# Layer-norm statistics of the last stage by bn_stats and Newton steps, and the output copy on ScalarE

## The chip, the core and the metric

The kernel runs on one core of a Trainium2 chip. The metric is the device time of one execution in microseconds (us), from runs on the chip. TensorE (PE) does matrix products and transposes, VectorE (DVE) elementwise work and sums, ScalarE (ACT) elementwise functions and copies, GpSimd (POOL) and SyncE (SP) issue DMAs. Each engine works off its own list of instructions in order and waits on semaphores of the others.

## The reference, cut to what matters

Two networks follow each other on a float32 tensor of shape (4, 64, 256, 256). The last stage of the kernel computes the second network's column attention and its feed-forward block. For every pixel `x` is a vector of E = 64 channels:

```
def ln(x, g, b):
    m = x.mean(-1); v = mean((x - m) ** 2, -1)
    return (x - m) / sqrt(v + 1e-5) * g + b

h = x + lin_attn(ln(x, cn_g, cn_b), col_wq, col_wk, col_wv, col_wo)
      # q, k = elu(.) + 1, one number per head and pixel; q over its mean, k over its sum;
      # k^T v over a column's 256 rows, then q times that, then col_wo
out = h + w2 @ gelu(w1 @ ln(h, fn_g, fn_b) + b1) + b2
```

So each pixel is normalized twice: once ahead of the scores `q` and `k`, once ahead of the feed-forward. The scales and shifts `g`, `b` and the first centring are folded into the weights (`cwt`, `cgt`, `w1`, `b1`), so the kernel needs the reciprocal root `rs` of the variance for the scores, and `(x - m) * rs` for the feed-forward.

## The kernel before, in words

The earlier stages compute the first network and the row attention; the change does not touch them. The last one, `stage_d`, goes over 32 tiles `h` (4 images, 8 groups of 32 columns). A tile has 128 partitions, `h[p, c, a, e]`: column `c` of 32, row half `a` of 2, channel `e` of 64; partition and `a` make the row. Tiles come from `hd` by four DMAs of SP, two tiles ahead, four buffers.

Three tiles are in work at once, in a loop over `n`:

- `scores(n + 1)`: eight passes `r`. `up(r)` turns four columns' `h` on TensorE (L1252), ScalarE copies them to `xT` (L1254), `score` multiplies with `cwt` (L1261), `back` turns the results on VectorE (L1266) into `qp`. Ahead of pass 0 and after pass 3 `spread` computes half the tile's sums of squares. At the end `rstd` gives `rs`; `qp` times `rs` plus the bias (L1291, L1292) goes through `feature`: the minimum with 0 on VectorE (`fe`, L711), the exp on ScalarE (L712); then `f` (L1300) and `kz` (L1302).
- `result(n)`: the product of `kz` and `h` (L1313), its sums `zm` and `z` (L1325, L1327), `zn` (L1332), turned (L1335, L1337), through `mix` (L718 to L726) to `bdm` (L1341). Then twice four matmuls of the bias (L1347) and of `bdm` (L1350), and eight adds into `h` in place (L1353), four for each row half `a`. Then for each half `hf` of the columns `spread` and `rstd`, and the products `xf` (L1362).
- the feed-forward of tile `n - 1`, in eight passes of four columns: `turn` two passes ahead (`xf` turned, L1372, copied by ScalarE to `xfT`, L1374), `first` one pass ahead (four matmuls with `w1`, L1383, and Gelu on ScalarE into `hg`, L1385), `second` (`h` turned into the bank, L1397, products with `w2` on top, L1400, and a copy with the bias `b2` to `st`, L1401). `st` is written with a step of 32 words. After eight passes four DMAs of GpSimd write `st` to the output.

`spread` makes, for 16 pixels of 64 channels per partition at a time: the sum (L1223), the centred values `xc` (L1225), the squares on ScalarE (L1227) and their sum (L1231). `rstd` takes a root on ScalarE (L1236) and a reciprocal on VectorE (L1238). ScalarE holds one table of functions at a time: the root, the exp and the Gelu each need another, and a load (ACT_TABLE_LOAD) stands in its list at each change.

TensorE's order is written out by hand in the loop (`tc.manual_schedule`); a scheduler orders the lists of the other engines by its own costs when the program is built. Matmul results go to six PSUM banks (`mm`) and two (`sm`); a bank is used again when the engine that reads it is done.

Of the kernel before, what the change touches and what calls it, by code (L numbers as in the profile page):

```python
# [8 lines left out]

F32 = mybir.dt.float32  # L10
AF = mybir.ActivationFunctionType
ALU = mybir.AluOpType
AX = mybir.AxisListType

C, H, W = 64, 256, 256
HW = H * W
NPAIR = H // 2
EPS = 1e-5
LN_S = 1.0 / C
# [230 lines left out]
def kernel(ctx: ExitStack, tc: tile.TileContext, x, packs, fd, out, off):  # L250
    nc = tc.nc
    B = x.shape[0]
    V, S, T, G, SY = nc.vector, nc.scalar, nc.tensor, nc.gpsimd, nc.sync
# [24 lines left out]
    eps_t = const.tile([128, 1], F32, name="eps_t")  # L278
# [18 lines left out]
    def bc(ap, n):  # L297

        return ap.unsqueeze(2).to_broadcast([ap.shape[0], ap.shape[1], n])
# [10 lines left out]
    def layernorm(pool, src, xc, g, bufs=None):  # L310

        s1 = pool.tile([128, g], F32, tag="ln_s", name="ln_s")
        V.tensor_reduce(s1, src, AX.X, ALU.add)
        V.scalar_tensor_tensor(xc, bc(s1, C), -LN_S, src, ALU.mult, ALU.add)  # L314
        sq = pool.tile([128, g, C], F32, tag="ln_sq", name="ln_sq", bufs=bufs)
        S.activation(sq, xc, AF.Square)  # L316
        s2 = pool.tile([128, g], F32, tag="ln_v", name="ln_v")
        V.tensor_reduce(s2, sq, AX.X, ALU.add)  # L318
        s3 = pool.tile([128, g], F32, tag="ln_d", name="ln_d")
        S.activation(s3, s2, AF.Sqrt, bias=eps_t, scale=LN_S)  # L320
        s4 = pool.tile([128, g], F32, tag="ln_r", name="ln_r")
        V.reciprocal(s4, s3)
        V.tensor_tensor(xc, xc, bc(s4, C), ALU.mult)


    sp1 = ctx.enter_context(ExitStack())
    p = sp1.enter_context(tc.tile_pool(name="pst", bufs=2))
    p1 = sp1.enter_context(tc.tile_pool(name="pst1", bufs=1))
# [14 lines left out]
    K = load_pack(p1, "s")  # L343
# [837 lines left out]
    def stage_d():  # L1181
        with ExitStack() as cs:
            p = cs.enter_context(tc.tile_pool(name="pd", bufs=2))
            p1 = cs.enter_context(tc.tile_pool(name="pd1", bufs=1))
            K = load_pack(p1, "d")
            cwg, cbq, cgg = attn_weights(p1, "col", K)

            t = mm()
# [5 lines left out]
            t = mm()  # L1194
# [6 lines left out]
            t = mm()  # L1201
# [12 lines left out]
                        SY.dma_start(h[:, 16 * j:16 * j + 16, rh, :], hd[b, rh * 128:(rh + 1) * 128, :, 2 * g + j, :])  # L1214
                return h

            def spread(h, ks, v):

                xcs, sqs = [], []
                for k in ks:  # L1220
                    src = h[:, 8 * k:8 * k + 8].rearrange("p c a e -> p (c a) e")
                    s1 = p.tile([128, 16], F32, tag="ln_s", name="ln_s")
                    V.tensor_reduce(s1, src, AX.X, ALU.add)  # L1223
                    xc = p.tile([128, 16, C], F32, tag="xc", name="xc")
                    V.scalar_tensor_tensor(xc, bc(s1, C), -LN_S, src, ALU.mult, ALU.add)  # L1225
                    sq = p.tile([128, 16, C], F32, tag="ln_sq", name="ln_sq")
                    S.activation(sq, xc, AF.Square)  # L1227
                    xcs.append(xc)
                    sqs.append(sq)
                for i, k in enumerate(ks):  # L1230
                    V.tensor_reduce(v[:, 16 * i:16 * i + 16], sqs[i], AX.X, ALU.add)  # L1231
                return xcs

            def rstd(v, n):
                s3 = p.tile([128, n], F32, tag="ln_d", name="ln_d")
                S.activation(s3, v, AF.Sqrt, bias=eps_t, scale=LN_S)  # L1236
                s4 = p.tile([128, n], F32, tag="ln_r", name="ln_r")
                V.reciprocal(s4, s3)  # L1238
                return s4

            def scores(n):
                h = hs[n]
                qp = p1.tile([128, 32, 32], F32, name="qp")
                v1 = p1.tile([128, 64], F32, name="v1")

                def up(r):
                    t = mm()  # L1250
                    for i in range(4):
                        T.transpose(t[:, i * 128:(i + 1) * 128], h[:, r * 4 + i].rearrange("p a e -> p (a e)"), ident)  # L1252
                    xT = p.tile([128, 512], F32, name="xT")
                    S.copy(xT, t)  # L1254
                    return xT

                def score(r, xT, qk):


                    for g in range(4):  # L1260
                        T.matmul(qk[g * 32:(g + 1) * 32, r % 4 * 128:r % 4 * 128 + 128], cwt, xT.rearrange("p (c n) -> p c n", c=4)[:, :, g * 32:(g + 1) * 32],  # L1261
                                 start=True, stop=True)

                def back(k, qk):

                    V.transpose(qp[:, k * 16:k * 16 + 16].rearrange("p c m -> p (c m)"), qk)  # L1266

                xT = up(0)
                yield
                yield  # L1270
                qk = sm()
                for r in range(8):
                    if r == 0:
                        spread(h, (0, 1), v1[:, 0:32])
                    if r == 4:
                        back(0, qk)
                        qk = sm()
                    score(r, xT, qk)
                    if r < 7:
                        xT = up(r + 1)  # L1280
                    if r == 3:
                        spread(h, (2, 3), v1[:, 32:64])
                    yield
                    if r == 1:
                        yield
                        yield

                back(1, qk)
                rs = rstd(v1, 64)
                u = qp[:, :, 0:16].rearrange("p c (r k) -> p c r k", r=2)  # L1290
                V.tensor_tensor(u, u, bc4(rs, 2, 8), ALU.mult)  # L1291
                V.tensor_tensor(u, u, cbq.unsqueeze(1).unsqueeze(1).to_broadcast([128, 32, 2, 8]), ALU.add)  # L1292
                e = feature(p1, u, [128, 32, 2, 8])
                yield
                f = p1.tile([128, 2, 2, 32, 4], F32, name="f")
                uv = u.rearrange("p c r k -> p r c k")
                ev = e.rearrange("p c r k -> p r c k")
                for rh in (0, 1):
                    for k in (0, 1):
                        V.scalar_tensor_tensor(f[:, rh, k], uv[:, rh, :, k * 4:k * 4 + 4], 1.0, ev[:, rh, :, k * 4:k * 4 + 4], ALU.add, ALU.max)  # L1300
                kz = p1.tile([128, 2, 128], F32, name="kz")
                V.tensor_tensor(kz.rearrange("p r (c h) -> p r c h", h=4), f[:, :, 1], rs.rearrange("p (c r) -> p r c", r=2).unsqueeze(3).to_broadcast([128, 2, 32, 4]), ALU.mult)  # L1302
                fks[n] = f, kz

            def result(n):
                h = hs[n]
# [46 lines left out]
                        V.tensor_tensor(hh, ts[g].rearrange("p (c e) -> p c e", c=8), hh, ALU.add)  # L1353
                    yield
                for hf in (0, 1):
                    v2 = p.tile([128, 32], F32, name="v2")
                    xcs = spread(h, (2 * hf, 2 * hf + 1), v2)
                    yield
                    rs = rstd(v2, 32)
                    for k in (0, 1):  # L1360
                        xf = p.tile([128, 8, 2, C], F32, name="xf", bufs=6)
                        V.tensor_tensor(xf.rearrange("p c a e -> p (c a) e"), xcs[k], bc(rs[:, k * 16:k * 16 + 16], C), ALU.mult)  # L1362
                        xfs[n, 2 * hf + k] = xf
                    yield
# [23 lines left out]
            def second(i):  # L1388

                n, r = divmod(i, 8)  # L1390
                h, hg = hs[n], hgs.pop(i)
                if r == 0:
                    sts[n] = p.tile([128, 128, 32], F32, name="st")
                st = sts[n]
                y = mm()
                for k in range(4):
                    T.matmul(y[:, k * 128:(k + 1) * 128], h[:, r * 4 + k].rearrange("p a e -> p (a e)"), ident, is_transpose=True, start=(k == 0), stop=False, skip_group_check=True)  # L1397
                for k in (0, 1):
                    for rh in (0, 1):
                        T.matmul(y[rh * 64:(rh + 1) * 64, :], w2[:, k, :], hg[k * 2 + rh], start=False, stop=(k == 1), skip_group_check=True)  # L1400
                V.tensor_scalar(st[:, :, 4 * r:4 * r + 4].rearrange("p r c -> p c r"), y.rearrange("p (c r) -> p c r", c=4), K("b2"), None, ALU.add)  # L1401
                if r == 7:
                    b, g = seq[n]
                    for q in (0, 1):
                        for rh in (0, 1):
                            y0 = rh * 128 + q * 64
                            G.dma_start(out[b, :, y0:y0 + 64, g * 32:g * 32 + 32], sts[n][rh * 64:(rh + 1) * 64, q * 64:(q + 1) * 64])  # L1407
                    del hs[n]
# [46 lines left out]
```

## Time and profile before

| what | value |
|---|---|
| times of three runs | 8467.74, 8469.86, 8471.41 us; median 8469.86 |
| span of the profiled execution | 8468.2 us, 1.7 below the median of the runs |
| granted TensorE clock, mean | 0.976 |
| TensorE busy | 7969.8 us, 94% |
| VectorE busy | 5829.9 us, 69% |
| ScalarE busy | 4723.4 us, 56% |
| last stage | from about 6351 us to the end |
| first and last `z` (L1327) of its 32 tiles | 6398.3 and 8367.5 us |

The profile is of one execution. Its views: the page; busy time by stretches; groups of instructions by line, shape and operation, with busy time, mean and idle time before them; waits by who waited for whom; the chain of work that ended last; the timeline, where a row gives start and duration, and `xN` merges N instructions. A duration reaches from an instruction's start to its end, and on VectorE and ScalarE the next often starts a little before that end. Lines (L1223) are those of the kernel before.

### The profile page before, as it was taken

What the parts mean: (1) busy time and instruction counts of PE and PEld (TensorE: products, weight loads), DVE (VectorE), ACT (ScalarE), POOL (GpSimd) and SP (SyncE); (2) the same over time, 40 slices, a digit from 0 to 9 for tenths busy, and PEclk for the clock granted to TensorE, in tenths of its full rate; (3) what the DMA queues carried; (4) which work ended last, traced back from release to release, by engine and by line L of the source; (5) the groups of instructions that cost most, each with busy time, mean ns of one, the idle gap of its engine ahead of it and who ended that gap; (6) DMA issues with size and microseconds to landing.
All of it is one profiled execution on the core that took longest, in us unless ns stands there. A gap on an engine that the chain in (4) does not pass through costs nothing.

```text
span 8468.2 us, 143522 instructions
## 1 busy us (share of the span) xinstructions
PE 7969.8 (94%) x57518; PEld 4144.7 (49%) x57518; DVE 5829.9 (69%) x8506; ACT 4723.4 (56%) x8297; POOL 1077.1 (13%) x1764
## 2 busy tenths in 40 slices
PE   8999998799999998999999999999987999999998
PEld 6877777344444443333333345555553444444443
DVE  7777775577777773222222278888877888888886
ACT  4466554455555553222222267777765777777776
POOL 1122221122222221000000001111110010010111
PEclk9999999799999999999999999999997999999999
DMA  7788886899999998888888866666642333333332
GB/s 164 169 217 218 214 209 164 278 391 389 388 389 392 394 383 303 299 296 295 298 298 299 278 208 187 193 187 194 186 130 64 64 76 60 68 73 60 72 69 40
DMA packets 1258505, 1832.50 MB, mean 216 GB/s; under 512 B 335600, under 2 KB 1040112, under 8 KB 1196656
## 3 DMA queue, kind: packets, MB, share of 16 engines
q1 hardware_dynamic: 1053296, 1034.63, 40.8%
q0 software_dynamic: 204544, 788.69, 29.3%
q8 instruction: 456, 7.47, 0.4%
q14 instruction: 209, 1.71, 0.1%
HBM read 967.65 MB, written 788.53 MB: 207 GB/s over the span
## 4 chain that ended last, share of the span: by engine, by line
PE 68%; ACT 15%; DVE 11%; issue 3%; DMA 2%; POOL 0%; SPq 0%; ACTq 0%; DVEq 0%; POOLq 0%
PE mm L898 13%; PE mm L630 8%; PE mm L905 6%; PE mm L791 4%; PE mm L840 3%; PE mm L1161 3%; PE mm L1383 3%; ACT xl L828 2%; ACT hg L1385 2%; PE mm L1400 2%; PE sm L617 2%; PE mm L1059 2%; DVE ln_s L1223 2%; PE mm L1030 2%; PE mm L986 2%
## 5 line engine op out<-in xcount | busy, mean ns | idle before, releaser
L931 DVE TENSOR_TENSOR y<-ge,mm 128x512 f32<-128x512 f32 (+1 forms) x640 | 405.9, 634 | 1213.7 <-ACT ge L930 1213.7
L898 PE MATMUL mm<-t,w 128*128 128x512 f32 (+1 forms) x2560 | 1094.7, 566 | 18.5 <-DMA t<-td 18.5
L930 ACT ACTIVATE ge<-mm 128x512 f32<-128x512 f32 (+1 forms) x640 | 354.7, 554 | 1253.8 <-PE mm L905 1253.8
L791 PE MATMUL mm<-gp,wc 128*64 128x510 f32 (+1 forms) x3072 | 702.2, 595 | 89.2 <-DVE xm L801 51.2
L898 PEld LDWEIGHTS mm<-t,w 128*128 128x128 f32 x2560 | 455.6, 190 | 647.5 <-issue 437.0
L630 PEld LDWEIGHTS mm<-wqk,gp 128*128 128x128 f32 x6144 | 705.8, 192 | 73.5 <-issue 66.2
L630 PE MATMUL mm<-wqk,gp 128*128 128x128 f32 x6144 | 738.5, 277 | 0.0
L1383 PE MATMUL mm<-xfT,w 64*128 64x512 f32 x2048 | 619.4, 640 | 51.3 <-ACT hg L1385 27.0
L1385 ACT ACTIVATE hg<-mm,b 128x512 f32<-128x512 f32 x1024 | 633.3, 687 | 54.0 <-PE mm L1383 52.4
L846 ACT COPY tb<-mm 128x512 f32<-128x512 f32 x512 | 300.3, 587 | 630.8 <-PE mm L840 622.7
L905 PE MATMUL mm<-t,w 64*64 64x504 f32 (+1 forms) x5120 | 575.6, 555 | 0.0
L840 PE MATMUL mm<-xl,pack_c 64*128 64x512 f32 x2048 | 511.4, 602 | 6.2 <-ACT xl L828 4.3
L791 PEld LDWEIGHTS mm<-gp,wc 128*64 128x64 f32 x3072 | 277.3, 137 | 468.8 <-issue 332.4
L1400 PE MATMUL mm<-hg,pack_d 128*64 128x512 f32 x2048 | 505.5, 615 | 0.0
L316 ACT ACTIVATE ln_sq<-xn 128x1024 f32<-128x1024 f32 x256 | 274.9, 1074 | 333.5 <-DVE xn L314 333.4
L1407 POOL DMA_DIRECT2D out_dram<-st x128 | 208.8, 1636 | 1759.0 <-DVE fe L711 1542.5
L318 DVE TENSOR_REDUCE ln_v<-ln_sq 128x16 f32<-128x1024 f32 x256 | 311.4, 1217 | 120.8 <-ACT ln_sq L316 120.8
L1401 DVE TENSOR_SCALAR st<-mm,pack_d 128x512 f32<-128x512 f32 x256 | 280.5, 1096 | 119.0 <-PE mm L1400 119.0
L844 DVE COPY tb<-mm 128x512 f32<-128x512 f32 x512 | 344.2, 683 | 24.2 <-PE mm L840 18.5
L1383 PEld LDWEIGHTS mm<-xfT,w 64*128 64x128 f32 x2048 | 224.3, 191 | 275.5 <-issue 124.8
L1227 ACT ACTIVATE ln_sq<-xc 128x1024 f32<-128x1024 f32 x256 | 272.9, 1067 | 132.7 <-DVE xc L1225 132.7
L905 PEld LDWEIGHTS mm<-t,w 64*64 64x64 f32 x5120 | 158.1, 132 | 374.4 <-issue 374.4
(458 smaller groups left out, 15158.3 us busy)
## 6 DMA issues: line engine op xcount, KB each, us to landing
t<-td SPq DMA_DIRECT2D x256, 1152.0 KB, 10.3
td<-tb POOLq DMA_DIRECT2D x144, 1024.0 KB, 15.3
td<-tb POOLq DMA_DIRECT2D x288, 512.0 KB, 13.5
yd<-y POOLq DMA_DIRECT2D x128, 1152.0 KB, 10.1
ya<-yd SPq DMA_DIRECT2D x192, 512.0 KB, 8.3
xs<-in_x_dram SPq DMA_DIRECT2D x128, 512.0 KB, 6.9
projd<-pj POOLq DMA_DIRECT2D x256, 256.0 KB, 5.4
gp<-projd SPq DMA_DIRECT2D x128, 512.0 KB, 9.2
```

The lines of the kernel that those rows point to most:

```text
L318: V.tensor_reduce(s2, sq, AX.X, ALU.add)
L630: T.matmul(qp[:, k * 128:(k + 1) * 128], gp[:, 2 * i + k // 2, at + dx:at + dx + 128], wqk[:, dx, :], start=(dx == 0), stop=(dx == 2))
L791: T.matmul(tv[i * 64:(i + 1) * 64, :, o], wc[2 * pr + i][:, dx, :], gps[i][:, 2 * r:2 * r + 2, i_], start=(dx == 1), stop=False, skip_grou ...
L840: T.matmul(t, inT[q, hf * 128:(hf + 1) * 128], xls[b // 2, s][q, :, 2 * y:2 * y + 2].rearrange("p f y t -> p f (y t)"), start=True, stop=True)
L844: V.tensor_copy(o, i_)
L898: T.matmul(t[:, :n], w[:, 0:128], x_[:, c, :], start=True, stop=False, skip_group_check=True)
L905: T.matmul(t[po:po + 64, :n].rearrange("p (n c) -> p n c", c=64)[:, :, o], w[q:q + 64, 128:192], x_[q:q + 64, c, i_], start=False, stop=Tr ...
L930: S.activation(ge[:, :n], ts[0][k][:, :n], AF.Gelu)
L931: V.tensor_tensor(y[:, c, :].rearrange("p n c -> p (n c)"), ge[:, :n], ts[1][k][:, :n], ALU.mult)
L1383: T.matmul(t, w1[rh * 64:(rh + 1) * 64, k * 128:(k + 1) * 128], xT[rh * 64:(rh + 1) * 64], start=True, stop=True)
L1385: S.activation(g, t, AF.Gelu, bias=b1[:, k:k + 1])
L1400: T.matmul(y[rh * 64:(rh + 1) * 64, :], w2[:, k, :], hg[k * 2 + rh], start=False, stop=(k == 1), skip_group_check=True)
```

## The change

In the last stage only:

- `spread` becomes `stats`: one `bn_stats` on VectorE for each pixel of a partition, 64 channels in and six numbers out (count, mean and sum of squared deviations of the even and of the odd elements). There are 128 for a tile, 64 ahead of the scores and 64 ahead of the feed-forward; squares on ScalarE and sums on VectorE are gone.
- `variance` joins the two halves in four small VectorE instructions, and `rsqrt` takes the reciprocal root with a first guess from the number's bits (two instructions) and three Newton steps (three each). No root and no table load for it are left on ScalarE.
- The scores no longer compute centred values. Ahead of the feed-forward one more small instruction makes twice the mean (`m2`), and `xc` is centred with it; this comes before the first `yield` of each half, the variance and root after it.
- The copy of the output bank to `st` with the bias `b2` moves from VectorE to ScalarE.

```
+    def variance(p, s6, n):
+        d = p.tile([128, n], F32, tag="va_d", name="va_d")
+        V.tensor_tensor(d, s6[:, :, 1], s6[:, :, 4], ALU.subtract)
+        V.scalar_tensor_tensor(d, d, 0.25, d, ALU.mult, ALU.mult)
+        v = p.tile([128, n], F32, tag="va_v", name="va_v")
+        V.scalar_tensor_tensor(v, s6[:, :, 2], C * EPS, s6[:, :, 5], ALU.add, ALU.add)
+        V.scalar_tensor_tensor(v, v, LN_S, d, ALU.mult, ALU.add)
+        return v
+
+    def rsqrt(p, v, n):
+        y = p.tile([128, n], F32, tag="rq_y", name="rq_y")
+        t = p.tile([128, n], F32, tag="rq_t", name="rq_t")
+        V.tensor_scalar(t.bitcast(I32), v.bitcast(I32), 1, None, ALU.logical_shift_right)
+        V.tensor_scalar(y.bitcast(I32), t.bitcast(I32), -1.0, float(0x5F3759DF), ALU.mult, ALU.add)
+        for k in range(3):
+            V.scalar_tensor_tensor(t, y, -0.5, y, ALU.mult, ALU.mult)
+            V.tensor_tensor(t, t, v, ALU.mult)
+            V.scalar_tensor_tensor(y, t, 1.5, y, ALU.add, ALU.mult)
+        return y
...
-            def spread(h, ks, v):
...
-            def rstd(v, n):
...
+            def stats(h, ks, s6):
                 for k in ks:
+                    for c in range(8):
+                        for a in (0, 1):
+                            V.bn_stats(s6[:, (k - ks[0]) * 16 + 2 * c + a, :], h[:, 8 * k + c, a, :])
...
-                v1 = p1.tile([128, 64], F32, name="v1")
+                s6 = p1.tile([128, 64, 6], F32, name="s6")
...
-                        spread(h, (0, 1), v1[:, 0:32])
+                        stats(h, (0, 1), s6[:, 0:32])
...
-                        spread(h, (2, 3), v1[:, 32:64])
+                        stats(h, (2, 3), s6[:, 32:64])
...
-                rs = rstd(v1, 64)
+                rs = rsqrt(p, variance(p, s6, 64), 64)
...
-                    v2 = p.tile([128, 32], F32, name="v2")
-                    xcs = spread(h, (2 * hf, 2 * hf + 1), v2)
-                    yield
-                    rs = rstd(v2, 32)
+                    s6 = p.tile([128, 32, 6], F32, name="s62")
+                    stats(h, (2 * hf, 2 * hf + 1), s6)
+                    m2 = p.tile([128, 32], F32, name="m2")
+                    V.tensor_tensor(m2, s6[:, :, 1], s6[:, :, 4], ALU.add)
+                    xcs = []
+                    for k in (0, 1):
+                        xc = p.tile([128, 16, C], F32, tag="xc", name="xc")
+                        src = h[:, 8 * (2 * hf + k):8 * (2 * hf + k) + 8].rearrange("p c a e -> p (c a) e")
+                        V.scalar_tensor_tensor(xc, bc(m2[:, k * 16:k * 16 + 16], C), -0.5, src, ALU.mult, ALU.add)
+                        xcs.append(xc)
+                    yield
+                    rs = rsqrt(p, variance(p, s6, 32), 32)
...
-                V.tensor_scalar(st[:, :, 4 * r:4 * r + 4].rearrange("p r c -> p c r"), y.rearrange("p (c r) -> p c r", c=4), K("b2"), None, ALU.add)
+                S.activation(st[:, :, 4 * r:4 * r + 4].rearrange("p r c -> p c r"), y.rearrange("p (c r) -> p c r", c=4), AF.Identity, bias=K("b2"))
```

More of the change, by code (lines that the diff above doesn't have):

```diff
@@ L10 @@
 F32 = mybir.dt.float32
+I32 = mybir.dt.int32
 AF = mybir.ActivationFunctionType
@@ L1215, in load @@
                 return h
-            def spread(h, ks, v):
-                xcs, sqs = [], []
+            def stats(h, ks, s6):
                 for k in ks:
[L1221 to L1232, printed above, removed]
-            def rstd(v, n):
[L1235 to L1239, printed above, removed]
+                    for c in range(8):
+                        for a in (0, 1):
+                            V.bn_stats(s6[:, (k - ks[0]) * 16 + 2 * c + a, :], h[:, 8 * k + c, a, :])
             def scores(n):
```

## The prediction

> **What bounds the kernel now.** I read the page first (which stage is which), then the stretches by stage, the VectorE groups of the last stage, the chain in order of time, and short timelines. The last stage runs from about 6351 us to the end. Its steady stretch:
>
> ```profile
> 6700.00:8300.00 1600.00, 1477.09 (x8795) 670.29 (x8794) 1368.40 (x1696) 1211.93 (x1747) 170.42 (x128) 0.98 0.34 67
> ```
>
> The columns are the stretch, its length, busy time of TensorE, its weight loads, VectorE, ScalarE and GpSimd, clock, DMA share and GB/s. TensorE is busy 92%, VectorE 86%, ScalarE 76%: no engine is full, so a loop of waits sets the pace. The stage makes 32 tiles, one a "round". The chain of work that ended last, in order of time (start, us, engine), shows one of them:
>
> ```profile
> 7305.44 0.68 DVE h L1353
> 7306.15 1.22 DVE ln_s L1223
> ...
> 7345.02 0.58 ACT hg L1385
> 7345.61 1.28 ACT L712
> 7346.91 0.64 ACT fe L712
> 7347.57 0.91 DVE f L1300 x4
> 7349.07 1.92 PE mm L1313 x16
> ...
> 7367.69 0.90 PE mm L1350 x8
> 7368.59 0.68 DVE h L1353
> ```
>
> From L1353 to the same L1353 is 63.2 us. First VectorE and ScalarE in turn (statistics, roots, exp), from the adds into `h` (L1353) to `f`; then TensorE alone, from the product of `kz` and `h` (L1313) to the adds of the next round. What the change buys or costs on VectorE counts in the first part alone. In the timeline the first of the eight adds starts at 7363.65, 14.6 us after L1313; so the first part, from first add to L1313, is 63.2 - 14.6 = 48.6 us.
>
> The VectorE groups of 6800 to 8000 us (19 rounds; busy us and mean ns, then idle):
>
> ```profile
> L1225 DVE SCALAR_TENSOR_TENSOR xc<-ln_s,h 128x1024 f32<-128x1024 f32 x152 | 182.8, 1213 | 0.0
> L1231 DVE TENSOR_REDUCE v<-ln_sq 128x16 f32<-128x1024 f32 x152 | 182.1, 1208 | 0.0
> L1223 DVE TENSOR_REDUCE ln_s<-h 128x16 f32<-128x1024 f32 x152 | 180.2, 1206 | 0.6
> L1401 DVE TENSOR_SCALAR st<-mm,pack_d 128x512 f32<-128x512 f32 x152 | 166.4, 1095 | 48.9 <-PE mm L1400 48.9
> ```
>
> Eight of each per round (152 in 19). A duration overlaps the next one's start: in the timeline two L1223 take 2.29 to 2.35 us and starts are 1.13 apart. I count these spacings.
>
> **Removed, per round.** VectorE: 8 sums (L1223), 8 sums of squares (L1231) and 4 of 8 centrings (L1225), 20 x 1.13 = 22.6 us; 8 copies to `st`, 8 x 0.95 = 7.6; 3 reciprocals, 1.1. Together 31.3. ScalarE: 8 squares at 0.97, 3 roots at 0.33, and 6 table loads of 1.28 (three to the root's table, three back; the pair around the exp stays): 16.4.
>
> **Added.** VectorE: 128 `bn_stats` of 64 columns, 45 small instructions (three chains of 15: 4 for the variance, 2 for the first guess, 9 for three Newton steps; two on 32 columns, one on 64) and 2 for the mean. ScalarE: 8 biased copies to `st`.
>
> The price of `bn_stats` decides all, and no row shows one. Nearest are two-input instructions on 64 columns, issued back to back:
>
> ```profile
> 5001.76 0.21 DVE L1103 TENSOR_TENSOR kj<-fr,pack_e 128x64 f32<-128x64 f32 x1
> 5001.89 0.21 DVE L1104 TENSOR_TENSOR qj<-fr,pack_e 128x64 f32<-128x64 f32 x1
> 5002.02 0.21 DVE L1103 TENSOR_TENSOR kj<-fr,pack_e 128x64 f32<-128x64 f32 x1
> 5002.16 0.21 DVE L1104 TENSOR_TENSOR qj<-fr,pack_e 128x64 f32<-128x64 f32 x1
> ```
>
> Spacing 0.133, duration 0.215. With 1.13 for 1024 columns that is 1.04 ns a column plus 0.066 fixed. Lower end: 0.133. Upper end: 0.215, no overlap with the next. I take 0.15, near the spacing, with some 16 columns more for six results instead of one and for keeping even and odd elements apart (an estimate). Small instructions by the same line: 0.10 on 32 columns, 0.133 on 64: 32 x 0.10 + 15 x 0.133 = 5.2 us. Their dependence is mostly covered, since the changed order puts a `bn_stats` between each two of a chain. So VectorE gets 128 x 0.15 + 5.2 = 24.4 for 31.3.
>
> [...]
>
> ScalarE's copy to `st` writes with a stride. Rows: `hg` (L1385), 512 columns written in order, 0.69; `xl` (L828), 256 columns written with a stride, 0.81, where a 256-column one in order would be near 0.47: 1.3 ns a column more, so up to 1.36 for 512; VectorE's own strided copy is 1.10 against 0.75 (L580). I take 1.04 (0.69 plus VectorE's difference), ends 0.70 and 1.36. ScalarE is 8.1 us a round lighter, but its order is what matters.
>
> **The new round.** TensorE's order is unchanged. On VectorE the changed order puts between the first add and `fe` (L711, the operand of the exp): 8 adds, 98 of the 128 `bn_stats`, all 47 small ones, 4 centrings, 4 products `xf`, 2 transposes, 2 operations on `qp`, `fe`; all ready, so VectorE runs without a gap. On ScalarE the exp now stands half a pass earlier: before it come two of the four `hg` of a `first`, behind it that pass's other two and an `st`. ScalarE will sit at the exp until `fe` is there, and TensorE, whose six `mm` banks then hold results nobody has taken, stands still at L1383. Then it has a backlog before L1313, with VectorE idle. The sum:
> - VectorE, first add to `fe`: adds 8 x 0.60, centrings and `xf` 8 x 1.13, transposes and `qp` 4 x 0.61, `fe` 0.43: 16.7; small ones 5.2; three waits of 0.1 and the strided columns of the statistics 0.5 (the strided sum `z` takes 1.02 against 0.69 for 512 columns); 98 x 0.15 = 14.7. Sum 37.1.
> - Relay: exp 0.65, table load 1.30, two `hg` 1.18, `st` 1.04, TensorE's start 0.2: 4.4.
> - TensorE's backlog to L1313: L1397 and L1400 twice (0.59 + 1.86 each), L1372 0.59, L1383 1.91, L1252 0.59: 8.0.
> - L1313 to first add, as now: 14.6.
>
> Total 64.1 against 63.2: +0.9 a round, x31 = +28. At the ends the statistics stand alone (the first `scores`: 12 passes at 1.13, root and two loads, near 16 us, against 64 x 0.15 + 15 x 0.2 = 12.6), some 3 us in each of the five rounds that lack part of the load: -14. Net +14. The profiled span is 8468.2; the median of the runs, 8469.9, lies 1.7 above. 8468.2 + 14 + 1.7 = 8484. So 7 us a round less work on VectorE and 8 on ScalarE come to nothing: they come back as the wait at the exp. TensorE's idle time in the groups of those 19 rounds is 91 us, 4.8 a round, which leaves 58.4 of its own; in a round of 64.1 it would stand 5.7. The output's four DMAs a round now wait for ScalarE instead of VectorE; `st` has two buffers and they land within 11.4 us, so they cost nothing while a round lasts longer.
>
> Each 0.01 us of `bn_stats` is 98 x 0.01 x 31 = 30 us; that makes the range. Measurement tells 0.2%, 17 us.
>
> **Rivals.**
> 1. Faster: `bn_stats` at the spacing of L1103, 0.133, and the `st` copy at 0.70. The first part of the sum gives -1.7 a round, the relay -0.34: 31 x (0.9 - 2.0) - 14 = -48, 8422. With the copy at 1.04, 8432. It decides below 0.14. For it: sums along the columns (L1223) cost no more than an elementwise pass. Against: six results.
> 2. Clearly slower, one mechanism: a `bn_stats` does not overlap the next, so the 98 between first add and `fe` cost 0.215 each, +6.4 a round; 31 x 7.3 - 14 = +212, 8682. With the copy at 1.36, 8692. It is slower by over 0.2% from 0.151 on. For it: it keeps state to the end of its row. Against: sums do that too and overlap.
> 3. The exp's wait hides: `fe` is ready before ScalarE arrives, TensorE never stands, and the round falls to TensorE's own work, 63.2 less its present stalls of 4.8: 58.4, or 8300. VectorE's stretch would have to be 5.7 us shorter, `bn_stats` near 0.09, under every row. Likewise that the roots' loads stay: no root is left on ScalarE.
>
> **How the numbers follow.** Forecast case (0.138 to 0.18): 0.45, own range 8447 to 8575. Rival 1: 0.24. Rival 2 (0.18 to 0.22): 0.20; beyond (several cycles per element) 0.09. Rival 3: 0.02. Range: 8425 (rival 1 with a dear or a cheap copy) to 8700 (rival 2), leaving out some 0.15. The limits of 17 us are 0.14 and 0.151. Faster: rivals 1 and 3 and a sliver, 0.28. Within: 0.18. Slower: 0.54; the forecast stands between, since the unknown price has more room upwards.
>
> **What would show it.** Rounds of 64 us between `z`s; `bn_stats` starting 0.15 apart; a ScalarE wait of several us at the exp; TensorE waiting as long at L1383's line for an `hg`, under 6 us idle a round in all; VectorE idle for some 8 us (the backlog) ahead of `zm`; two table loads a round. Wrong if rounds are under 62 or over 66 us, if VectorE has gaps between first add and `fe`, or if TensorE waits elsewhere.

## The result, and the profile after

The changed kernel takes 8488.76 us (median of 20 runs, 8483.38 to 8496.82), the kernel before 8469.85 (20 runs, 8461.39 to 8478.69): a ratio of 1.0021, 95% interval 1.0014 to 1.0028. The spans are 8489.9 and 8468.2. The forecast was 8484.

Lines have moved: bn_stats is L1246, the adds into `h` L1357, `hg` L1397 with its product L1395, `fe` L735 and the exp L736, the copy to `st` L1413 with its products L1409 and L1412, the product of `kz` and `h` L1317, `zm` L1329.

The same stretch of the last stage as before (stretch, length, busy time and count of TensorE, its weight loads, VectorE, ScalarE, GpSimd; clock, DMA share, GB/s):

```profile
6700.00:8300.00 1600.00, 1480.32 (x8647) 646.64 (x8645) 1087.99 (x5172) 990.18 (x1481) 165.56 (x125) 0.95 0.32 66
```

VectorE and ScalarE are relieved as intended: 1088 us busy for 1368, and 990 for 1212. TensorE is as busy as before with fewer instructions, and its mean clock fell from 0.98 to 0.95. The next view shows where. One round of the chain that ended last, in order of time (start, us, engine):

```profile
7304.60 0.68 DVE h L1357
...
7334.41 2.54 DVE s L1246 x20
...
7339.16 0.34 DVE fe L735
7339.55 0.62 issue
7340.17 1.28 ACT L1397
7341.46 0.70 ACT hg L1397
7342.20 2.65 PE mm L1395 x4
7344.85 1.04 PE mm L1409 x4
7345.90 3.61 PE mm L1412 x8
7349.51 0.61 PE mm L1384 x4
7350.12 1.92 PE mm L1395 x8
...
7353.06 1.87 PE mm L1412 x8
7354.92 1.85 PE mm L1317 x16
...
7369.45 0.68 DVE h L1357
```

From L1357 to L1357 is 64.85 us (63.2 before). Twenty bn_stats take 2.54 us, 0.127 each. Compare the two L1412: eight matmuls take 3.61 us at 7345.90 and 1.87 at 7353.06. They are the same instructions, and TensorE's timeline has no wait in either; the granted clock differs. In the windows around TensorE's stand (a "stand" is a time in which TensorE has nothing it may start; columns as above):

```profile
7337.00:7342.20 5.20, 1.01 (x4) 0.18 (x4) 5.20 (x28) 2.65 (x4) 0.00 (x0) 1.00 0.00 0
7342.20:7349.40 7.20, 7.20 (x16) 2.27 (x16) 2.23 (x15) 4.29 (x7) 0.00 (x0) 0.53 0.35 81
7349.50:7356.00 6.50, 6.50 (x42) 2.82 (x44) 0.00 (x0) 5.51 (x8) 4.87 (x3) 1.00 1.26 284
```

TensorE is busy for 1.01 of 5.20 us, and then runs at 0.53 of its clock for 7.2 us. The output's DMAs do not slow it: in the last row they move 284 GB/s and the clock is 1.00, in the slow stretch they move 81. The waits of 6800 to 8000 us, 19 rounds (us in total, times, longest):

```profile
DVE zm L1329 <- PE mm L1317: 223.5, 18, 12.4
PE mm L1395 <- ACT hg L1397: 79.7, 19, 4.2
ACT fe L736 <- DVE fe L735: 73.6, 19, 3.9
```

Read from the bottom: ScalarE waits 3.9 us at the exp, TensorE therefore 4.2 us for a free `mm` bank, and VectorE later 12.4 us for the backlog. These are the three waits forecast; the slow backlog was not.

The trace has a record of the granted clock, with the start and length of every stretch at half clock. Every kernel of this document has one or two long ones at the start of the last stage, over by 6435 us. Behind them and up to the last `z`, the changed kernel falls to half clock 30 times, each time for 6.83 us, 205 us in all; the kernel before 21 times, 102 us in all. The eight L1412 above take 3.61 us at half clock for 1.87, so about half of such a time is lost, and each 6.83 us costs up to 3.4 us where TensorE is the path.

### The profile page after: what moved, and what is told of

It is laid out like the page before. It is cut to its first block, busy times and chain, and to the rows that moved or that the text cites. A ratio compares the mean times of both kernels' runs of the same rounds, so it can differ in the third digit from the quotient of the medians.

```text
span 8489.9 us, 147627 instructions
## 1 busy us (share of the span) xinstructions
PE 8010.2 (94%) x57518; PEld 4130.9 (49%) x57518; DVE 5512.6 (65%) x13114; ACT 4482.4 (53%) x8013; POOL 1077.1 (13%) x1764
## 4 chain that ended last, share of the span: by engine, by line
PE 68%; DVE 17%; ACT 10%; issue 2%; DMA 2%; POOL 0%; SPq 0%; DVEq 0%; POOLq 0%; ACTq 0%
PE mm L922 13%; PE mm L654 8%; PE mm L929 6%; DVE s L1246 5%; PE mm L815 4%; PE mm L1395 3%; PE mm L864 3%; PE mm L1412 3%; PE mm L1185 3%; ACT xl L852 2%; DVE h L1357 2%; PE mm L1083 2%; PE sm L641 2%; DVE xc L1368 2%; DVE xf L1374 2%
## 5 line engine op out<-in xcount | busy, mean ns | idle before, releaser
L1395 PE MATMUL mm<-xfT,w 64*128 64x512 f32 x2048 | 623.7, 644 | 145.9 <-ACT hg L1397 122.2
L1397 ACT ACTIVATE hg<-mm,b 128x512 f32<-128x512 f32 x1024 | 633.3, 689 | 126.9 <-PE mm L1395 123.2
L1246 DVE BATCH_NORM_STATS2 s<-h 128x6 f32<-128x64 f32 x4096 | 629.0, 211 | 2.2
L1412 PE MATMUL mm<-hg,pack_d 128*64 128x512 f32 x2048 | 548.3, 660 | 0.0
L1413 ACT ACTIVATE st<-mm,pack_d 128x512 f32<-128x512 f32 x256 | 295.6, 1155 | 397.5 <-PE mm L1412 397.5
L1395 PEld LDWEIGHTS mm<-xfT,w 64*128 64x128 f32 x2048 | 203.8, 189 | 375.2 <-ACT hg L1397 156.4
## 6 DMA issues: line engine op xcount, KB each, us to landing
yd<-y POOLq DMA_DIRECT2D x128, 1152.0 KB, 10.1
```

The costliest lines, as they stand in the source:

```text
L1246: V.bn_stats(s6[:, (k - ks[0]) * 16 + 2 * c + a, :], h[:, 8 * k + c, a, :])
L1395: T.matmul(t, w1[rh * 64:(rh + 1) * 64, k * 128:(k + 1) * 128], xT[rh * 64:(rh + 1) * 64], start=True, stop=True)
L1397: S.activation(g, t, AF.Gelu, bias=b1[:, k:k + 1])
```

## The experiments

"Round" in this table is the mean distance of the 32 sums `z`, read from the first and the last start of their group. "Half clock" is the time at half clock in the falls behind the stage's start and up to the last `z`, from the clock record. The ratio is to the kernel before, run again beside each group of experiments (medians 8469.9 to 8474.0 us), with its 95% interval.

| kernel | median us | ratio | round us | half clock us |
|---|---|---|---|---|
| before | 8469.9 | | 63.52 | 102 |
| after | 8488.8 | 1.0021 (1.0014 to 1.0028) | 64.13 | 205 |
| 1: 8 fillers | 8508.7 | 1.0040 (1.0027 to 1.0052) | 64.32 | 92 |
| 2: 3, and the exp later | 8291.5 | 0.9783 (0.9770 to 0.9797) | 57.84 | 102 |
| 3: ScalarE in program order | 8343.9 | 0.9849 (0.9835 to 0.9862) | 59.53 | 109 |
| 4: copy on VectorE | 8498.5 | 1.0029 (1.0018 to 1.0041) | 64.52 | 215 |
| 5: 4 fillers | 8406.5 | 0.9922 (0.9909 to 0.9934) | 61.50 | 68 |
| 6: root on ScalarE | 8390.6 | 0.9904 (0.9888 to 0.9919) | 60.85 | 41 |
| 7: before, copy on ScalarE | 8484.2 | 1.0015 (1.0006 to 1.0024) | 63.72 | 89 |
| 8: 2, statistics twice | 8449.9 | 0.9976 (0.9966 to 0.9985) | 63.03 | 249 |
| 9: 2, root on ScalarE | 8437.4 | 0.9961 (0.9948 to 0.9975) | 62.51 | 133 |
| 10: 2, one filler | 8249.1 | 0.9737 (0.9724 to 0.9751) | 56.44 | 7 |

My theory after the comparison was: ScalarE's place for the exp makes TensorE stand, and the stand costs twice, by itself and by the half clock behind it. The rivals: the half clock is hidden and the stand alone counts; the moved copy is what costs.

**1 and 5: fill the stand.** In `first`, for the pass whose third bank TensorE waits for:

```diff
                     for rh in (0, 1):
+                        if i % 8 == 7 and (k, rh) == (1, 0):
+                            fill = sm()
+                            for _ in range(8):        # 4 in the second run
+                                T.matmul(fill, w1[0:64, 0:128], xT[0:64], start=True, stop=True)
                         t = mm()
```

> The changed kernel with eight unneeded matmuls of 512 columns (their results are read by nobody) between the second and the third product of the pass in which TensorE stood still for 4.2 us a round. Theory: TensorE's standing still costs a second time, because its granted clock is at half (0.53) for the 7.2 us after it; kept busy (8 x 0.48 = 3.8 us), it keeps its clock, the stall shrinks to under 1 us, and a round falls from 64.9 to about 61.5 us, the kernel to about 8390 us. Rival: the slow matmuls after the stall come from something else (the output's DMAs run at the same time, or banks); then more work for TensorE leaves rounds at 64.9 or lengthens them, 8490 us or more.

Missed: 8508.7, slower than the changed kernel. A T.matmul becomes two matmuls of 0.43 us here, so the filler lasted 6.75 us, 2.6 more than the stand that it was to fill. It did halve the half clock (205 to 92 us), but gave that back. I had sized the filler without working out its length. With half as many:

> The changed kernel with filler products on TensorE where it stands ahead of L1395, now half as many: 4 products, 8 matmuls of 0.43 us as the run with 16 showed, 3.4 us in all, inside the stand of 4.19 us. Their result is read by nobody. With 16 the filler took 6.75 us, 2.6 more than the stand, and the mean clock rose from 0.95 to 0.98; so that run hid its own gain. Theory (the half clock behind the stand costs about 3 us a round): the filler costs nothing, the clock stays near 1.00 behind it, the mean clock of the stretch is 0.98 again, and a round gets 0.03 x 65 = 2 to 3 us shorter: 8395 to 8430. Rival (the stand sets the end and the half clock is hidden, or so little filler does not hold the clock): 8480 to 8495.

8406.5, inside the range; a round's filler now takes 3.4 us. The windows of one round of this kernel, the filler and then the backlog:

```profile
7224.00:7227.50 3.50, 3.50 (x13) 1.64 (x11) 3.50 (x22) 2.55 (x3) 0.00 (x0) 1.00 0.00 0
7227.50:7235.00 7.50, 7.50 (x37) 3.01 (x36) 6.33 (x40) 6.05 (x9) 0.00 (x0) 1.00 0.00 1
```

The backlog behind the filler runs at 1.00. This kernel does strictly more work than the changed one and is 82 us faster: the half clock behind the stand lies on the path. Of the 102 us that it could cost at 30 x 3.4, this run won back 82; its own 68 us of half clock lie elsewhere, most of them behind the wait of 0.8 us at the adds (last section). Of the two fillers tried, the one shorter than the stand won and the longer one lost.

**2 and 3: take the stand away.** In 3 ScalarE's list is in program order instead of the scheduler's (the last line of the edit); in 2 the exp is also two half-passes later (the two `yield`):

```diff
             def scores(n):
                 ...
+                yield
+                yield
                 e = feature(p1, u, ...)
 ...
-            with tc.manual_schedule(engines={mybir.EngineType.PE}):
+            with tc.manual_schedule(engines={mybir.EngineType.PE, mybir.EngineType.Activation}):
```

> The changed kernel, with ScalarE's list in the order of the program text instead of the scheduler's, and the exp two half-passes later in it. The arithmetic is the same. Theory: the lighter statistics were worth several us a round and were lost to the place of the exp in ScalarE's list; with the exp behind work that is ready, TensorE stands still for 2 to 3 us a round only (behind VectorE's adds), its clock stays whole, and a round falls to 57 to 59 us, the kernel to 8270 to 8340 us. Rival: VectorE's stretch of 34.9 us sets the round by itself; then the place of the exp matters little and rounds stay above 63 us, 8430 or more.

> As the kernel with the late exp, but the exp where the program text has it, behind all four Gelu results of its pass instead of two of four. Theory: this alone gives TensorE two more results to go on with, so that the stall falls under 3.4 us; a round of 59 to 61 us, the kernel 8330 to 8400. Rival (VectorE's stretch alone): above 63 us a round, 8430 or more.

Both inside their ranges: 8291.5 and 8343.9. In 3 TensorE still waits 1.4 us a round, at most 2.4, for the copy to `st` (27.8 us in all from 6800 to 8000 us), and has 109 us of half clock: no run shows the 3.4 us of its expectation as a limit. The waits of 2 in the same stretch, about 21 rounds:

```profile
PE mm L1397 <- DVE h L1359: 16.1, 21, 0.8
DVE zm L1331 <- PE mm L1319: 90.2, 20, 4.9
```

TensorE no longer waits for an `hg` bank (its product is L1397 in this kernel); what is left is 0.8 us at the adds, and VectorE waits 4.5 us for `zm` instead of 12.4. One part of the theory missed: 2 to 3 us of stand and a whole clock were expected, and behind the 0.8 us there are still 102 us of half clock (run 10). No instruction was removed: ScalarE's order is worth 197 us. The two half-passes of the exp are 52 of them; the other 145 came with the whole list in program order, where more than the exp moves. That they too are the exp's place is read from the waits, and was not tested apart.

**4 and 7: the copy to `st` alone.** 4 puts it back on VectorE in the changed kernel, 7 makes this one change in the kernel before:

```diff
-                V.tensor_scalar(st[...], y..., K("b2"), None, ALU.add)
+                S.activation(st[...], y..., AF.Identity, bias=K("b2"))
```

> The changed kernel with the copy to the output tile back on VectorE; the scheduler may order the lists anew. Theory: the copy's place is no lever: it takes 7.6 us a round off ScalarE and puts as much into VectorE's stretch between the first add and the exp's operand; rounds near 64.3 us, the kernel 8470 to 8500. Rival: the copy on ScalarE (1.155 us each, behind the exp and ahead of TensorE's next bank) is where the gain went; then rounds fall under 62 us, the kernel under 8420.

> The kernel before with one part of the change alone: the biased copy of the output tile on ScalarE. VectorE loses 7.6 us a round, ScalarE gains 8 copies of 1.16, 9.2 us, and was busy 76%. Theory (what VectorE gives up ahead of the exp is paid back as ScalarE's copies ahead of the same exp): a round within 1 us of 63.2, 8440 to 8500. Rival (this copy alone undoes the change, since ScalarE's order holds TensorE's banks): 65.5 or more a round, over 8540. Rival 2 (VectorE's time counts in full): 60 a round, 8370 or less.

Both times lie in the theory's ranges. 8498.5 is not told from the changed kernel, since the intervals of the two ratios overlap, and 8484.2 is 14 us more than before. The copy's move by itself brings nothing measurable on top of the other changes, and costs a little without them. In the changed kernel one copy costs ScalarE 1.156 us (mean of 149, 6800 to 8000 us).

**6: the root back on ScalarE.** In `rsqrt` of the changed kernel:

```diff
-        (first guess and three Newton steps)
+        s3 = p.tile([128, n], F32, tag="ln_d", name="ln_d")
+        S.activation(s3, v, AF.Sqrt)
+        s4 = p.tile([128, n], F32, tag="ln_r", name="ln_r")
+        V.reciprocal(s4, s3)
```

> The changed kernel with the reciprocal root made as before the change (root on ScalarE, reciprocal on VectorE) in place of the first guess and three Newton steps; statistics and copy as changed. VectorE loses 33 small instructions a round, some 3.7 us, and gains 3 reciprocals, 1.1; ScalarE gains 3 roots of 0.33 and table loads of 1.28 around them. Theory (the round is VectorE's run up to the exp's operand, and ScalarE waits there 3.9 us): roots and loads fit into ScalarE's waits, VectorE's run is some 2.5 us shorter, and with it the stand of TensorE and its half clock: 8390 to 8440. Rival (the steps on VectorE were worth it, because a root on ScalarE stands in front of copies that TensorE waits for): 8520 to 8600.

8390.6: the time at the lower edge of the range, the reason only half right. VectorE's run from the first add (7191.34) to the end of `fe` (7225.76) is 34.4 us, hardly under the 34.9 of the changed kernel. The bn_stats inside that run, first here and then in the changed kernel:

```profile
L1242 DVE BATCH_NORM_STATS2 s<-h 128x6 f32<-128x64 f32 x119 | 16.6, 212 | 0.1
```

```profile
L1246 DVE BATCH_NORM_STATS2 s<-h 128x6 f32<-128x64 f32 x99 | 15.8, 211 | 0.1
```

The scheduler filled the place of the Newton steps with 20 more statistics: 20 x 0.127 = 2.5 us, what had come out. The gain is on TensorE, in its timeline (start, us, idle before in brackets):

```profile
7228.47 1.70 PE L1391 MATMUL mm<-xfT,w 64*128 64x512 f32 x4 [1.22 <-ACT hg L1393]
```

It stands 1.22 us for 4.19, and the clock does not fall: its four matmuls take 1.70 for 2.65, and from its start to the product of `kz` and `h` pass 9.5 us for 12.7. ScalarE waits 0.9 us at the exp for 3.9. TensorE waits 1.5 us a round more for ScalarE at other places (L1261 for `xT`), so both come to the exp later; that the roots' table loads do this is my reading of their order, and was not tested apart.

6, 7 and the changed kernel give the price of each part, one on top of the other: the copy on ScalarE +14 (8484.2 for 8469.9), bn_stats for sums and squares -94 (8390.6), Newton steps for the roots +98 (8488.8). Each has an uncertainty of some 10 to 15 us, by the intervals of the ratios.

**8 and 9: two prices with the exp late.** 8 does the statistics of the results a second time, 64 bn_stats a round into a tile that is not read; 9 makes the roots on ScalarE, as in 6.

```diff
                     stats(h, (2 * hf, 2 * hf + 1), s6)
+                    s6b = p.tile([128, 32, 6], F32, name="s6b")
+                    stats(h, (2 * hf, 2 * hf + 1), s6b)
```

> The version with the exp late and ScalarE in program order (8291), with the 64 statistics of the results in each round done a second time into a tile that nobody reads. 64 x 0.127 = 8.1 us more VectorE a round, of which VectorE had 4.9 us to spare ahead of zm. Theory (there a round is TensorE's own work, and VectorE's run decides again when it exceeds its spare time): 8.1 - 4.9 = 3.2 us a round more, 31 x 3.2 = 100: 8370 to 8420. Rival (VectorE's run counts in full there too): 8291 + 31 x 8.1 = 8542. Rival 2 (TensorE alone counts): 8291 to 8310.

8449.9, past the range: a round is 5.2 us longer, not 3.2. The waits of TensorE and the windows of 8 say why:

```profile
PE mm L1399 <- DVE h L1359: 60.2, 19, 3.2
PE mm L1319 <- DVE kz L1308: 21.5, 15, 2.1
```

```profile
6800.00:8000.00 1200.00, 1112.49 (x6643) 508.61 (x6643) 996.42 (x5242) 762.31 (x1141) 125.89 (x95) 0.94 0.32 68
```

The stand at the adds grew from 0.8 to 3.2 us, 2.4 a round. TensorE now also waits ahead of the product of `kz` and `h` (L1319), for `kz` and a few times for `xT` (5.7 us in all), 1.4 a round. And its busy time is 58.4 us a round for 57.3: the half clock grew from 102 to 249 us, so that the same matmuls take longer. Together 4.9 of the 5.2. The expectation had priced neither the half clock nor the wait for `kz`.

> The version with the exp late and ScalarE in program order (8291), with the reciprocal root made by ScalarE's root and VectorE's reciprocal in place of the Newton steps. In the changed kernel that swap brought 98 us (8390 for 8489), since ScalarE had a wait of 3.9 us at the exp for it to fill. Theory (with the exp late that wait is gone, so roots and six table loads a round now stand in front of copies that TensorE waits for, and VectorE's lighter run buys nothing): 60 to 62 a round, 8340 to 8420. Rival (the Newton steps are a loss wherever they stand): 8190 to 8280.

8437.4: the theory's direction, 17 us past its range; 146 us slower than the same kernel with Newton steps. Now VectorE waits for ScalarE, and TensorE too (19 rounds):

```profile
DVE f L1302 <- ACT fe L732: 88.7, 19, 4.7
PE sm L1261 <- ACT xT L1254: 52.4, 38, 1.6
```

So the same exchange of roots for Newton steps costs 98 us in one order of ScalarE and brings 146 in another.

**10: fill the stand that is left.** One product in 2, ahead of the second bank of the pass behind the adds:

```diff
+                        if i % 8 == 4 and (k, rh) == (0, 0):
+                            fill = sm()
+                            T.matmul(fill, w1[0:64, 0:128], xT[0:64], start=True, stop=True)
```

> The version with the exp late (8291), with one filler product (2 matmuls of 0.43 us, read by nobody) on TensorE where it still stands 0.8 us a round, after the first L1397 product behind the adds. There its clock falls to half in about two rounds of three: 126 us of half clock in the stage, 63 us lost if all of it is on the path. Theory (a stand as short as this one triggers it, and TensorE's own work is the round): the filler fills the stand and the half clock goes, up to 2.0 us a round: 8230 to 8270. Rival (0.8 us of filler changes nothing in what triggers the half clock): 8285 to 8300, or 8318 if the filler adds to TensorE's work.

8249.1, inside the range, the fastest of all: 0.9737 of before. (The clock record of 2 has 18 falls and 102 us in 31 rounds, not the 126 us of the expectation.) TensorE waits for nothing in the stretch, and the clock stays up:

```profile
6800.00:8000.00 1200.00, 1200.00 (x7428) 540.00 (x7427) 933.50 (x4473) 846.23 (x1267) 139.24 (x105) 1.00 0.36 75
```

One fall behind the stage's start is left. In run 2 a round without a fall takes 56.65 us, one with 3.41 us of half clock 58.2 and one with 6.83 us 59.6 to 59.9; in run 10 every steady round takes 56.65. So the gain of 42 us is the half clock. With TensorE busy throughout, the round is now TensorE's own work.

## Why the prediction was right, and where its sum was not

The time was 4.8 us from the forecast. The mechanism was the one forecast, but that the time came so close is luck: two terms of the sum were wrong, by about -70 and +96 us, and with the ends (-15) they nearly cancelled.

**What held.** The mechanism: VectorE runs without a gap from the first add to `fe`; ScalarE stands at the exp (3.87 us); TensorE stands for an `hg` bank (4.19 us, 4.95 with the wait at the adds; under 6 was said); there are two table loads of 1.28 us a round (eight before, one at each change between root, exp and Gelu); the round of 64.85 stands against 64.1. L1317 to the first add is 14.5 us (14.6). Runs 2 and 3 show that ScalarE's order is the cause: in another order the stand for `hg` and the loss are gone. The output's DMAs cost nothing, as said: they land within 12.1 us.

**The price of bn_stats** was too high: 0.127 us, under the lowest row (0.133), for 0.15. Six results instead of one added nothing, so the 16 extra columns of the estimate were wrong. 98 x 0.023 = 2.25 us a round, 70 us in 31 rounds; VectorE's run is 34.9 for 37.1.

**The half clock was missing.** The sum gave TensorE's backlog its full-clock durations, though the prediction had TensorE standing 5.7 us a round written down, ahead of that backlog above all. First add to `fe` 34.9 (37.1), relay to L1409 5.4 (4.4), backlog to L1317 10.1 (8.0), the rest 14.5 (14.6): together 64.9. The second and third terms are 3.1 too small, 96 us in 31 rounds; against run 6, which runs the same matmuls at full clock, they lose 1.0 in L1395, 0.4 in L1409 and 1.7 in L1412. The clock record of the changed kernel has it in every steady round: TensorE stands for 4.19 us, and from 0.5 us behind the end of that stand its clock is half for 6.83; the last section has shorter waits that do the same. A sign was at hand in the trace of before, and the prediction should have weighed it: its clock record has 3.41 us of half clock in every second steady round, with no wait of TensorE over 2.0 us.

Without that cost the changed kernel would have been faster, as Rival 1 had it: the limit that the prediction set for it, a bn_stats under 0.14, was met. Run 5, where the fillers hold the clock up behind the stand, shows it: 8406.5, less than before.

**Rival 3** was put at 0.02 because VectorE's run would have to be 5.7 us shorter. Another order of ScalarE (run 2) came to the same from the other side. Its floor of 58.4 us a round for TensorE was too high as well: it was taken from 6800 to 8000 us of the kernel before, where the clock record has nine events of 3.41 us, 9 x 1.7 / 19 = 0.8 us lost a round. Run 10's steady round is 56.65, filler included; where the remaining 1 us comes from stays open.

**The copy** to `st` took 1.156 for 1.04; it stands once in the relay, so that is 0.1 a round at most. (The 0.47 us that its upper end was worked out from is above the rows of 256 columns in order, 0.37 to 0.42.) **VectorE idle ahead of `zm`** was to be 8 us and is 12.4. The 8 were the backlog alone; it is 2.1 us longer, and `zm` also waits for the product L1317 itself, 1.9 us, which I had not counted.

**The ends**: steady rounds cost 31 x 1.65 = +51 (+28 said). The first distance of two `z` is 49.6 us (61.9 before) and the last 57.7 (67.3 before), and ahead of the first and behind the last `z` 2.8 us are lost. With the early rounds, which are longer before, the ends come to 21.7 - 51 = -29, for -14 said. That too cancelled.

## What to carry to other kernels

When a change makes TensorE stand longer, price the stand and the matmuls behind it: here 4.2 us of stand cost some 3 more through the clock, and a few matmuls that nobody reads, no longer than the stand, won back 82 us. Where an engine's order decides which wait comes last, the price of one part has no sign of its own: Newton steps for roots cost 98 us with the exp early and brought 146 with it late, so look first at where the exchanged work stands in the lists. A forecast that lands can hold two wrong terms; only the segments of the chain, set beside the sum, show it.

## What the runs showed of the hardware that was not expected

The half clock comes in whole steps. In the clock record all 30 falls of the changed kernel last 6.83 us, twice 3.41, and from the second on they come 64.85 us apart, 19 times 3.413; those of the kernel before last 3.41, 6.83 and once 20.48 us. In every trace here the falls behind the stage's start begin on a grid of 3.413 us (in the kernels before and after none is off it by more than 0.002 us). A steady round of a whole number of its steps suggests that the round has locked onto this grid, and run 4, with other work on VectorE and ScalarE, has the same steady round of 64.85 us and the same 6.83 us in each; it was not tested apart.

A stand far shorter than a step can be enough. In run 2 TensorE waits 0.8 us at the adds, its only wait, and falls to half clock in more than every second round (windows around that wait):

```profile
7214.00:7220.00 6.00, 5.39 (x30) 1.80 (x30) 6.00 (x35) 2.31 (x3) 0.00 (x0) 1.00 0.00 0
7220.20:7229.20 9.00, 9.00 (x34) 3.62 (x38) 9.00 (x47) 2.65 (x4) 0.00 (x0) 0.62 0.00 0
```

Run 10, which fills this wait with one product, removes nearly all of it (7 us of half clock for 102), so the wait is the trigger. The changed kernel has the same wait of 0.8 us without a fall of the clock there. The clock record tells the cases apart by where the wait lies in the grid of 3.413 us. In run 2, from 6500 us on, 17 of these waits begin within 1.4 us of a grid point, and all 17 are followed by half clock from the next grid point on; the other 13 begin 1.6 us or more behind a grid point, and none is. Runs 1 and 5 go the same way, run 1 with two exceptions. In the changed kernel, whose round is 19 steps of the grid, the wait begins 2.1 to 2.6 us behind a grid point every time. How much of a step is idle does not decide it alone: in the changed kernel the long stand leaves 1.3 us of one step idle and 2.9 of the next, no step throughout, and the clock falls only behind the second. Why the place counts stays open.

Last, bn_stats on 64 columns starts every 0.127 us when one follows another, no dearer than a plain two-input instruction on them (0.133), with six results written; and its duration of 0.21 us overlaps the next.
